# A pre-norm attention and mixture-of-experts layer: where GpSimd makes the router's constants, and three small moves

## The chip, the core and the metric

The kernel runs on one core of one Trainium2 chip. A core has five engines that run side by side, each through its own queue in order: TensorE (matmuls; PE in the profile, with its weight loads as PEld), VectorE (DVE), ScalarE (ACT), GpSimd (POOL) and SyncE (SP, which here only issues transfers). All data is float32; each matmul or transpose of the program shows as two instructions on TensorE. The metric is the device time of one execution in microseconds. Three executions of the kernel before took 1071.76, 1071.80 and 1072.09 us; the median is 1071.8.

## The reference

x has 4096 tokens of width 256. First an attention over normalized rows is added to x, then a mixture of experts over the normalized result:

```python
x = x + attn(layernorm(x), Qw, Kw, Vw)      # causal, one head of width 256
x = x + ffn(layernorm(x), W_in, b_in, W_gate, ...)

def attn(x, Qw, Kw, Vw):
    Q, K, V = x @ Qw, x @ Kw, x @ Vw
    scores = Q @ K.T / sqrt(256) + causal_mask
    return softmax(scores) @ V

def ffn(...):
    t = x @ W_in + b_in
    probs = softmax(t @ W_gate + b_gate)        # 8 experts
    topv, topi = top_k(probs, 2); topv /= topv.sum()
    mid = relu(t @ W1[e] + b1[e]); eout = mid @ W2[e] + b2[e]
    return (sum over the two experts of topv * eout) @ W_out + b_out
```

## The kernel before

The tokens are handled in 8 blocks of 512 (NB = 8), each of four tiles of 128 rows (TPB = 4); queries are handled in 16 groups of 256 (g from 0 to 15). The engines' order is chosen by a scheduler when the program is built, from what is ready by its own estimate. Two calls bind it: `tc.keep_in_program_order(ins)` puts an instruction behind the one that was traced before it on its engine, and `tc.issue_after(ins)` puts all that a block traces on the engine of `ins` behind `ins`. Neither is a wait for data.

**The start.** The transfers are issued by SyncE: the first block of x, W_in, W_gate, the rows of biases `brows` (b1 and b_in, 66 rows of 128), Vw, the other blocks of x, and small rows. Qw and Kw come by ScalarE's queue. TensorE first runs some matmuls of zeros (L115), then turns Qw and Kw (L494), which ScalarE copies to qwT and kwT (L495). `turn_weights` turns the biases (L191, pbias, copied to biasT) and W_in (L198, pwin, copied to winT). Then comes the first of two products pqk (L502), and between the two, as `turn_first`, W_in times W_gate (L229, pwg) and the turn of the first block's normalized rows (L306, pz), pinned in this order; then the second product, and `project(0)` (L522), which makes the first block's queries.

**Normalized rows.** VectorE takes statistics of a tile (L254, L255), GpSimd adds epsilon (L261) and raises to the power -1/2 (L262), and VectorE makes the rows z (L271), each a tensor_scalar of 128 x 256 with a mean and a factor per row. In the first block this is done in two pairs of tiles (`first_rows`), pinned; in the others in fours. The second block's statistics and factors (`stats0(1)`) are put behind the last copy of the first projection.

**GpSimd's constants.** Beside the identity and the mask, GpSimd makes what the router will need: a strictly triangular matrix `before` (a memset and an affine select), 24 small memsets (rank, first, number), `none`, two iotas and a memset (blocks, assign), and the tiles `empty` (128 x 256) and `zero` (128 x 256), from which SyncE fills the tables `slots` and the last part of `rows` in memory. The columns of ones of the eight value tiles v are made in `values` (L533), one memset each. Nothing binds the place of any of them on GpSimd.

**The attention.** For each group g, `scores(g)` makes the scores in chunks of 256 keys (L566, ps), with a running maximum on VectorE (top, L600 to L605). Its `finish` turns top (L612, pt), reduces it (L617, m), turns that to a row for all partitions (L622, pmax), subtracts (L626, L632) and takes exponents. `attend(g)` multiplies with v (L647, po), and its `between` runs parts of other work behind the matmuls of a chunk. The scores of group g + 1 are made ahead of attend(g). For g below CALM = 4 `finish` is called at once, free to be placed by the scheduler; from 4 on it stands in `between`, its first turn pinned.

**The end.** When the experts' parts are added up, `gather` turns each block's sums (L1215, pa) into two tiles of PSUM, ScalarE copies both (L1220, aT), and `leave` multiplies with W_out (L1229, pf).

Of the kernel before, what the change touches and what calls it, by code (L numbers as in the profile page):

```python
# [10 lines left out]
F32 = mybir.dt.float32  # L11
I32 = mybir.dt.int32
# [5 lines left out]
P = 128  # L18
# [19 lines left out]
def preln_attention_moe_kernel(  # L38
# [145 lines left out]
    biasT = const.tile([P, NBR], F32, tag="biasT", name="biasT")  # L184
    winT = []

    def turn_weights():

        ptb = ps_tr("pbias")
        tc.keep_in_program_order(  # L190
            nc.tensor.transpose(ptb[:, :NBR], brows, ident[:NBR, :NBR])  # L191
        )
        nc.scalar.copy(biasT, ptb[:, :NBR])
        winT.append(piece("winT", ND, D))
        pt = ps_o("pwin")
        for k in range(ND):
            for c in range(ND):
                done = nc.tensor.transpose(  # L198
                    pt[:, ts(k * ND + c, P)], win_sb[:, c, ts(k, P)], ident
                )  # L200
                tc.keep_in_program_order(done)
        nc.scalar.copy(winT[0].rearrange("p k d -> p (k d)"), pt)
# [46 lines left out]
    def freely(done):  # L249
        return done  # L250

    def ln_stats(k, t, keep=freely):
        st = stats.tile([P, 6], F32, tag="bn", name=f"bn{k}_{t}")
        keep(nc.vector.bn_stats(out=st, in_=xb[t // TPB][:, t % TPB, :]))  # L254
        keep(nc.vector.bn_aggr(out=lns[k][0][:, t, :], in_=st))  # L255

    def ln_rstd(k, b, tiles=TPB, keep=freely):

        s = ts(b, tiles)
        mv, rstd = lns[k]  # L260
        keep(nc.gpsimd.tensor_scalar_add(rstd[:, s, 0], mv[:, s, 1], EPS))  # L261
        keep(nc.gpsimd.tensor_tensor(rstd[:, s, 0], rstd[:, s, 0], half[:, s], ALU.pow))  # L262

    def ln_rows(k, b, fill=None):

# [21 lines left out]

    def first_rows():

        todo, keep = [], tc.keep_in_program_order  # L290
        z = ln_rows(0, 0, todo)
        for i in range(TPB // 2):
            for j in range(2):
                ln_stats(0, 2 * i + j, keep)
            ln_rstd(0, i, 2, keep)
        for do in todo:
            keep(do())
        return z
# [177 lines left out]
    def piece(name, *shape):  # L476

        return attn.tile([P, *shape], F32, tag="s", name=name, bufs=NS)
# [33 lines left out]
    def stats0(b):  # L512
        for t in range(b * TPB, (b + 1) * TPB):
            ln_stats(0, t)
        ln_rstd(0, b)

    def project(b):
        qT[b] = attn.tile([P, ND, TB], F32, tag="qT", name=f"qT{b}", bufs=2)
# [11 lines left out]
        return done  # L530

    def values(b):
        nc.gpsimd.memset(vb[b][:, :, D : D + 1], 1.0)  # L533
        for j in range(TPB):
            pv = ps_o(f"pv{b}_{j}")
            for c in range(ND):
                nc.tensor.matmul(
                    pv[:, :D],
                    lhsT=zT[b][:, j, c, :],
                    rhs=vw_sb[:, c, :],  # L540
                    start=(c == 0),
                    stop=(c == ND - 1),
                )
            nc.scalar.copy(vb[b][:, j, :D], pv[:, :D])
# [488 lines left out]
    z, gates = first_rows(), []  # L1033

    def turn_first():
        gates.append(prepare_gate())
        turn(0, 0, z, zT[0], True)

# [3 lines left out]
    with tc.issue_after(ready.ins):  # L1042
        nc.vector.tensor_copy(
            win_sb[:, :, D:], gates[0][:, : ND * NE].rearrange("p (c e) -> p c e", e=NE)
        )
        stats0(1)

    before = const.tile([P, P], F32, tag="before", name="before")
    make_upper_triangular(nc, before, 1.0, diag=False)

    rank = const.tile([P, TPB, NE], F32, tag="rank", name="rank")

    first = const.tile([P, TPB, NE], F32, tag="first", name="first")
    number = const.tile([P, NE], F32, tag="number", name="number")
    for e in range(NE):
        nc.gpsimd.memset(rank[:, :, e : e + 1], float(NE - e))
        nc.gpsimd.memset(first[:, :, e : e + 1], float(e * R))
        nc.gpsimd.memset(number[:, e : e + 1], float(e))
    none = const.tile([P, SU], I32, tag="none", name="none")
    nc.gpsimd.memset(none, NONE)  # L1060
    late_slot = const.tile([P, SU], I32, tag="late_slot", name="late_slot")
    blocks = const.tile([P, NFULL], F32, tag="blocks", name="blocks")
    nc.gpsimd.iota(
        blocks, [[1, NFULL]], base=0, channel_multiplier=0, allow_small_or_imprecise_dtypes=True
    )


    assign = const.tile([P, NT * TOPK + LINE], I32, tag="assign", name="assign")
    nc.gpsimd.memset(assign[:, NT * TOPK :], NONE)
    nc.gpsimd.iota(  # L1070
        assign[:, : NT * TOPK].rearrange("p (t k) -> p t k", k=TOPK),
        [[TOPK * P, NT], [1, TOPK]],
        base=0,
        channel_multiplier=TOPK,
    )
    empty = attn.tile([P, SB], I32, tag="s", name="empty", bufs=NS)
    nc.gpsimd.memset(empty, NONE)
    nc.sync.dma_start(
        out=slots.rearrange("(p n r) o -> p n (r o)", p=P, r=SB // LINE),
        in_=empty.unsqueeze(1).to_broadcast([P, NE * R // P * LINE // SB, SB]),  # L1080
    )
    zero = piece("zero", D)
    nc.gpsimd.memset(zero, 0.0)

    nc.sync.dma_start(
        out=rows[TOPK * (S - LATE * TB) :, :].rearrange("(t p) d -> p t d", p=P),
        in_=zero.unsqueeze(1).to_broadcast([P, TOPK * (LATE * TPB + 1), D]),
    )

    row, finish = scores(0)  # L1090
    finish()
# [4 lines left out]
    for g in range(NT // KU):  # L1096
        b, q = divmod(g, QPB)

        between = {}
        nxt = None  # L1100
        if g + 1 < NT // KU:

            nxt, finish = scores(g + 1, fill)
            if g < CALM:
                finish()
            else:
                between[min(g - 2, 4)] = [partial(finish, True)]
        fill = []
        if q == 0 and b == NB - 1:

            assert not puts
            early = seen
            tables["a"] = plan("a", early, NFULL, SB, 0)
            for n in range(AHEAD + 1):
                got[n] = fetch_rows(work[n])
        if q == 0 and b > 0:

            def send(behind=False, b=b):
                nonlocal lg
                lg = enter(b - 1, z1T, attn, behind)  # L1120

            if b - 1 >= EASY[1]:
                between[5] = [partial(send, True)]
        if q == 0 and b == NB - 1:

            def fetch_first():
                for n in range(AHEAD):
                    got[n] += fetch_weights(work[n])

            def find():  # L1130
                nonlocal seen
                seen = route(b - 1, lg, seen, attn, True)
                while puts:
                    puts.pop(0)()

            between[6], between[11] = [fetch_first], [find]
            weighed = AHEAD
        elif g == 0:
            turn(0, 1, ahead, zT[1])
        late = q == 1 and 0 < b <= EASY[1]  # L1140
        if late:
            send()
        attend(g, row, between)
        row = nxt
        if q == 0 and b + 1 < NB:
            project(b + 1)
            values(b + 1)
        if late or q == 0 and EASY[1] < b < NB - 1:
            seen = route(b - 1, lg, seen, attn)
        if q == 0 and b + 2 < NB:  # L1150
            stats0(b + 2)
            todo = []
            todo += turn_todo(zT[b + 2], ln_rows(0, b + 2, todo))
            if b + 2 >= EASY[0]:
                fill += todo
            else:
                for do in todo:
                    do()
        if q == QPB - 1:
            ln_rstd(1, b)  # L1160
            z1T = attn.tile([P, TPB, ND, P], F32, tag="z1T", name=f"z1T{b}", bufs=1)
            todo = []
            rows1 = ln_rows(1, b, todo)
            if b < NB - 1:
                todo += turn_todo(z1T, rows1)
            if EASY[1] <= b < NB - 1:
                fill += todo
            else:
                for do in todo:
                    do()  # L1170
# [36 lines left out]
    def gather(b):  # L1207

        pts = [ps_tr(f"pa{b}_{c}") for c in range(ND)]
        if b > 0:  # L1210
            add_up(b)
        for i in range(2):
            for j in range(HT):
                for c in range(ND):
                    nc.tensor.transpose(  # L1215
                        pts[c][:, ts(i * HT + j, P)], accs[b, i][:, j, ts(c, P)], ident
                    )
        aT = [piece(f"aT{b}_{c}", TB) for c in range(ND)]
        for c in range(ND):
            nc.scalar.copy(aT[c], pts[c])  # L1220
        return aT

    def leave(b, aT):
# [127 lines left out]
```

## Time and profile before

| what | us |
|---|---|
| median of three executions | 1071.8 |
| the profiled execution | 1071.8 |
| its span, first to last instruction | 1070.0 |
| TensorE busy | 1062.0 (99%) |
| VectorE busy | 675.2 (63%) |
| ScalarE busy | 332.4 (31%) |
| GpSimd busy | 237.8 (22%) |

The profile is that of one execution. A busy time is the union of an engine's instructions; those of TensorE overlap, and their ends are modelled, so that what TensorE loses is better read from the starts of its instructions. A timeline line gives the start and the duration in us, the engine, the line of the code, the operation, what it writes and reads, the shapes and how many instructions were merged into the line; in brackets stands the idle time of the engine ahead of it and what ended it. Small differences of time in this text are taken from the starts of single instructions in the same trace.

### The profile page before, as it was taken

Reading aid. Unit: us, or ns where it says so; the run is one execution under the profiler, and the core shown is the slowest. Engines: PE = TensorE matmul, PEld = TensorE weight load, DVE = VectorE, ACT = ScalarE, POOL = GpSimd, SP = SyncE. Lnnn points to the kernel's source line nnn. Section 1 sums busy time; section 2 is a strip of 40 time slices with the busy share of each in tenths; the row PEclk is TensorE's granted clock in tenths of the full one; section 3 lists DMA queues with packets and bytes.
Section 4 is the critical chain, followed back from the end, with each engine's and each line's share of the span. In section 5 each row is a group of like instructions: output and inputs, shape, how many; then the busy total and the mean of one; then the engine's idle time right before and its main releaser. Section 6 shows DMA issues by size and latency. Waiting matters only on the chain. (4 is left out here: it accounts for less than half of the span.)

```text
span 1070.0 us, 15840 instructions
## 1 busy us (share of the span) xinstructions
PE 1062.0 (99%) x4973; PEld 882.8 (83%) x4973; DVE 675.2 (63%) x2158; ACT 332.4 (31%) x734; POOL 237.8 (22%) x289
## 2 busy tenths in 40 slices
PE   9999999999999999999999999999999999999998
PEld 6788888888888888888888887777878787777887
DVE  5877667564655546254665634858588786767636
ACT  2232233322432323242402221232323332323254
POOL 2102123202201110200223323232322322313110
PEclk9999999999999999999999999999999999999999
DMA  9431212121021011001655339887889796969285
GB/s 313 104 59 37 61 21 51 19 54 23 7 48 22 8 21 39 3 2 20 203 170 182 120 107 319 260 290 266 280 270 313 259 330 219 330 217 331 72 296 191
DMA packets 177994, 158.80 MB, mean 148 GB/s; under 512 B 82157, under 2 KB 157874, under 8 KB 177908
## 3 DMA queue, kind: packets, MB, share of 16 engines
q1 hardware_dynamic: 168980, 139.67, 41.8%
q0 software_dynamic: 8384, 17.58, 5.1%
q8 instruction: 40, 0.66, 0.2%
q10 hardware_dynamic: 544, 0.52, 0.1%
q14 instruction: 46, 0.38, 0.1%
HBM read 124.79 MB, written 26.38 MB: 141 GB/s over the span
## 5 line engine op out<-in xcount | busy, mean ns | idle before, releaser
L647 PE MATMUL po<-v,s 128*128 128x257 f32 x1056 | 237.9, 380 | 0.0
L566 PE MATMUL ps<-qT,zT 128*128 128x256 f32 x1088 | 233.3, 374 | 0.0
L566 PEld LDWEIGHTS ps<-qT,zT 128*128 128x128 f32 x1088 | 203.1, 190 | 28.0 <-issue 1.0
L647 PEld LDWEIGHTS po<-v,s 128*128 128x128 f32 x1056 | 197.2, 190 | 26.7
L575 ACT COPY s<-ps 128x512 f32<-128x512 f32 x120 | 70.2, 585 | 171.9 <-PE ps L566 129.1
L1004 PE MATMUL pe_a<-w_a,mid_a 128*128 128x256 f32 x544 | 121.6, 380 | 0.0
L935 PE MATMUL pm_a<-hT_a,w_a 128*128 128x256 f32 x544 | 120.0, 379 | 0.0
L1004 PEld LDWEIGHTS pe_a<-w_a,mid_a 128*128 128x128 f32 x544 | 102.6, 190 | 19.0 <-issue 5.6
L944 ACT ACTIVATE mid_a<-pm_a,c_a 128x256 f32<-128x256 f32 x136 | 63.8, 472 | 166.6 <-PE pm_a L935 125.7
L935 PEld LDWEIGHTS pm_a<-hT_a,w_a 128*128 128x128 f32 x544 | 103.4, 190 | 14.1
L581 DVE TENSOR_TENSOR mx<-ps,mx 128x512 f32<-128x512 f32 x91 | 62.9, 692 | 81.9 <-ACT s L575 75.4
L629 ACT ACTIVATE s<-s 128x512 f32<-128x512 f32 x120 | 72.3, 630 | 100.2 <-DVE s L626 100.2
L392 POOL DMA_INDIRECT slots<-assign,ati x64 | 63.5, 992 | 132.7 <-DVE ati L391 118.5
L915 DVE STREAM_TRANSPOSE hT_a<-h_a 32x128 f32<-32x128 f32 x272 | 82.2, 302 | 5.5 <-issue 1.7
L626 DVE TENSOR_TENSOR s<-s,pmax 128x512 f32<-128x512 f32 x120 | 73.1, 681 | 7.3 <-PE pmax L622 7.3
L1014 POOL DMA_INDIRECT parts<-y_a,slot_a x34 | 34.2, 1005 | 155.8 <-DVE y_a L1012 126.3
L907 DVE STREAM_TRANSPOSE mid_c<-raw_c 32x256 f32<-32x256 f32 x128 | 55.8, 436 | 1.9
L1004 PE MATMUL pe_b<-w_b,mid_b 128*128 128x256 f32 x256 | 56.8, 380 | 0.0
L935 PE MATMUL pm_b<-hT_b,w_b 128*128 128x256 f32 x256 | 56.6, 379 | 0.0
L1004 PEld LDWEIGHTS pe_b<-w_b,mid_b 128*128 128x128 f32 x256 | 48.5, 190 | 9.4 <-issue 3.1
L935 PEld LDWEIGHTS pm_b<-hT_b,w_b 128*128 128x128 f32 x256 | 48.6, 190 | 6.6
L944 ACT ACTIVATE mid_b<-pm_b,c_b 128x256 f32<-128x256 f32 x64 | 30.1, 471 | 63.0 <-PE pm_b L935 62.1
(281 smaller groups left out, 1169.3 us busy)
## 6 DMA issues: line engine op xcount, KB each, us to landing
w_a<-in_L_ffn_W_dram SPq DMA_DIRECT2D x68, 512.0 KB
w_d<-in_L_ffn_W_dram SPq DMA_DIRECT2D x48, 512.0 KB
w_c<-in_L_ffn_W_dram SPq DMA_DIRECT2D x32, 512.0 KB
w_b<-in_L_ffn_W_dram SPq DMA_DIRECT2D x32, 512.0 KB
rows<-hr SPq DMA_DIRECT2D x16, 512.0 KB
yp<-parts SPq DMA_DIRECT2D x14, 512.0 KB
x<-in_L_attn_x_dram SPq DMA_DIRECT2D x7, 512.0 KB
z1T<-z SPq DMA_DIRECT2D x112, 32.0 KB
```

The source lines that it names most:

```text
L392: put = nc.gpsimd.indirect_dma_start(out=slots, out_offset=bass.IndirectOffsetOnAxis(ap=ati, axis=0), in_=assign[:, TOPK * (b * TPB + j) + ...
L566: nc.tensor.matmul(ps[:, u * QB + lo : (u + 1) * QB], lhsT=zT[kt // TPB][:, kt % TPB, d, :], rhs=qT[b][:, d, q * QB + lo : (q + 1) * QB], ...
L575: nc.scalar.copy(flat, ps)
L581: done = nc.vector.tensor_tensor(mx, ps, old, ALU.max)
L626: nc.vector.tensor_tensor(s, s, pm[:, :QB].unsqueeze(1).to_broadcast([P, KU, QB]), ALU.subtract)
L629: nc.scalar.activation(s, s, AF.Exp)
L647: nc.tensor.matmul(po[u][:, : D + 1], lhsT=ss[c][:, k, ts(u, P)], rhs=vb[kt // TPB][:, kt % TPB, :], start=(kt == 0), stop=(kt == g * KU + u),
L907: pin(do())
L915: pin(do())
L935: nc.tensor.matmul(pm[:, :SB], lhsT=w1[c][:, ts(f, P)], rhs=hT[:, c, :], start=(c == 0), stop=(c == ND - 1),)
L944: nc.scalar.activation(mid[f // 2][:, f % 2, :], pm[:, :SB], AF.Relu, bias=c1[:, f : f + 1])
L1004: nc.tensor.matmul(pe[ts(j, rest), :D], lhsT=mid[f][:, ts(u, P)][:, ts(j, rest)], rhs=w2[f // (NF // 2)][:, f % (NF // 2), :], start=(f == 0),
```

## The change

- `turn_weights` is split. The biases' turn, now `turn_biases`, is called at the head of `turn_first`: behind the first product pqk and ahead of W_in times W_gate.
- `stats0` and `ln_rstd` return their last instruction, the power on GpSimd. All the router's constants, the fills of slots and rows, and the memsets of v's ones (now eight in one place, taken out of `values`) are traced under `issue_after` of the second block's power. The fills are SyncE's and so aren't bound by it, but they read what GpSimd makes there.
- For g = 2, `finish` of the fourth group (g + 1 = 3) isn't called at once but in `between[2]`: behind the last matmuls of attend(2), with its first turn pinned.
- In `gather`, for the first block alone, the second of the two copies is VectorE's.

```diff
-    def turn_weights():
-
+    def turn_biases():
         ptb = ps_tr("pbias")
         tc.keep_in_program_order(
             nc.tensor.transpose(ptb[:, :NBR], brows, ident[:NBR, :NBR])
         )
         nc.scalar.copy(biasT, ptb[:, :NBR])
+
+    def turn_weights():
+
         winT.append(piece("winT", ND, D))
...
+    def in_order(done):
+        tc.keep_in_program_order(done)
+        return done
+
...
-        keep(nc.gpsimd.tensor_tensor(rstd[:, s, 0], rstd[:, s, 0], half[:, s], ALU.pow))
+        return keep(
+            nc.gpsimd.tensor_tensor(rstd[:, s, 0], rstd[:, s, 0], half[:, s], ALU.pow)
+        )
...
-        todo, keep = [], tc.keep_in_program_order
+        todo, keep = [], in_order
...
-        ln_rstd(0, b)
+        return ln_rstd(0, b)
...
     def values(b):
-        nc.gpsimd.memset(vb[b][:, :, D : D + 1], 1.0)
...
     def turn_first():
+        turn_biases()
         gates.append(prepare_gate())
         turn(0, 0, z, zT[0], True)
...
-        stats0(1)
-
-    before = const.tile([P, P], F32, tag="before", name="before")
-    make_upper_triangular(nc, before, 1.0, diag=False)
...
+        second = stats0(1)
+
+    with tc.issue_after(second.ins):
+        for v in vb:
+            nc.gpsimd.memset(v[:, :, D : D + 1], 1.0)
+        before = const.tile([P, P], F32, tag="before", name="before")
+        make_upper_triangular(nc, before, 1.0, diag=False)
...
-            if g < CALM:
+            if g < CALM and g != 2:
                 finish()
             else:
-                between[min(g - 2, 4)] = [partial(finish, True)]
+                between[2 if g == 2 else min(g - 2, 4)] = [partial(finish, True)]
...
         for c in range(ND):
-            nc.scalar.copy(aT[c], pts[c])
+            if b == 0 and c:
+                nc.vector.tensor_copy(aT[c], pts[c])
+            else:
+                nc.scalar.copy(aT[c], pts[c])
         return aT
```

The lines between `before` and the fill of `rows` are the same on both sides, indented.

## The prediction

> **What bounds the kernel.** First the page: TensorE is busy 1062.0 us of a span of 1070.0 us and its clock is never reduced, so the end moves only by what TensorE waits for. (The profiled execution took 1071.8 us, which is also the median: 1.8 us lie outside the span, and a change of the span is a change of the time.) So next the list of TensorE's waits; its columns are the total, the number and the longest, in us.
>
> ```profile
> PE pbias L191 <- DMA brows<-in_L_ffn_b_dram: 1.1, 1, 1.1
> ...
> PE pt L612 <- DVE top L603: 1.0, 1, 1.0
> PE pf L1229 <- ACT aT L1220: 0.6, 1, 0.6
> ```
>
> These three waits are at 6.6, 51.3 and 1032.2 us, and each is touched by one part of the change. The fourth part, GpSimd's constants, is seen in the timeline of the start (start, duration, engine, line, out<-in):
>
> ```profile
> 6.89 1.48 DVE L271 TENSOR_SCALAR z<-x,ln0mv,ln0rstd 128x256 f32<-128x256 f32 x2
> 7.01 0.36 POOL L261 TENSOR_SCALAR ln0rstd<-ln0mv 128x2 f32<-128x2 f32 x1 [0.56 <-DVE past L441]
> 7.31 0.10 POOL L1056 MEMSET rank<- 128x4 f32 x1
> ...
> 8.12 0.09 POOL L1060 MEMSET none<- 128x2 int32 x1
> 8.18 0.24 POOL L1063 IOTA blocks<- 128x17 f32 x1
> ...
> 8.60 0.71 POOL L262 TENSOR_TENSOR ln0rstd<-ln0rstd,half 128x2 f32<-128x2 f32 x1
> ...
> 9.35 1.45 DVE L271 TENSOR_SCALAR z<-x,ln0mv,ln0rstd 128x256 f32<-128x256 f32 x2 [0.98 <-POOL ln0rstd L262]
> ```
>
> The second pair of factors has its addition at 7.01 but its power only at 8.60: 28 constants stand between. And VectorE's two rows take 1.48 and 1.45 us a pair, where three take 1.05 us later on. The query of that line says the same (minimum/median/maximum, ns):
>
> ```profile
> L271 DVE TENSOR_SCALAR z<-x,ln0mv,ln0rstd x32: 396/405/1153, 6.9 to 336.9; 128x256 f32<-128x256 f32 x32
> ```
>
> Exactly two of the rows are long (1153 and 1129 ns), the two that overlap runs of GpSimd constants. The first ends at 8.36, just after the run of memsets passes over into the iota (8.18); the second begins at 9.35 and ends at 10.48, 0.15 us after the last memset.
>
> **Part 1, biases' turn behind the first product; part 2, constants out of the first block.** Before, TensorE ends the turn of Kw near 6.6, waits for brows to 7.71, spends 0.09 us on it, and has W_in's turn at 7.80, the first product pqk at 8.24, pwg at 9.10 and the turn of z at 9.99. After, W_in's turn comes first; the DMA records signal the last part of win at 6.81, so it runs 6.85 to 7.29 (four turns of 0.109). The product needs kwT, whose copy ends at 7.28, so it starts at 7.33 instead of 8.24. Four matmuls of 0.215 and the biases' turn (brows is there since 7.7) put pwg at 7.33 + 0.86 + 0.09 = 8.28, 0.82 earlier. The turn of z is at 8.28 + 0.89 = 9.17. It took 1.13 us because the last rows came late; eight turns of 0.109 are 0.87. Are the rows there? Without the constants the power runs 7.45 to 8.17, and rows three and four end near 8.95: yes. So the second product starts at 10.04 where it stood at 11.12: **1.08 us gained**, carried on by the projection, since zT's copies follow the turn as before. Bounds: 0.8 (if rows are late by another reason) to 1.1.
>
> **Part 2, the other end: where the constants go.** They now follow the second block's power on GpSimd. Before:
>
> ```profile
> 18.67 1.04 POOL L262 TENSOR_TENSOR ln0rstd<-ln0rstd,half 128x4 f32<-128x4 f32 x1
> ...
> 19.75 0.41 DVE L271 TENSOR_SCALAR z<-x,ln0mv,ln0rstd 128x256 f32<-128x256 f32 x1 [0.62 <-POOL ln0rstd L262]
> ...
> 20.08 0.28 DVE L605 TENSOR_TENSOR top<-top,s 128x128 f32<-128x128 f32 x1
> 20.28 1.05 DVE L271 TENSOR_SCALAR z<-x,ln0mv,ln0rstd 128x256 f32<-128x256 f32 x3
> 20.41 0.14 PEld L612 LDWEIGHTS pt<-ident,top 128*128 128x128 f32 x1 [0.52 <-DVE top L605]
> ```
>
> The four rows wait for the same power. GpSimd's next instruction starts with no gap (9.29 after a power that ended at 9.31), VectorE's first row 0.04 us later. So 2.5 us of constants (7.31 to 8.61, 9.29 to 10.33, and 0.19 for the memset at 5.55) start just ahead of the rows. Behind the first row on VectorE stands L605, for which TensorE's second pt waits with no margin; behind the other rows stands the reduction m (L617, 21.25), for which pmax waits (21.90, margin 0.2).
>
> How long is a row held? The Trainium skill, page "SBUF — State Buffer", section "Who interferes with whom", says that a VectorE tensor_scalar in a two-port mode and a GpSimd instruction exclude each other, the first to issue keeping the port for its whole instruction; it also says that an operation with two inputs in SBUF, as L605 is, isn't held by a mere write. It speaks against this change. Held for one memset (0.1 us), four rows would lose at most some 0.4 us. The rows say more: a row waited for the whole run, 28 constants or 0.9 us, and lost 0.73 us; small memsets follow each other every 0.033 us and leave no opening. I take the row. In program order the run up to the first iota is v's 0.3, the mask's 0.45, then 0.85: the first row of block 1 ends some 1.7 us after the power instead of 0.45, L605 and the second pt are late by 1.25, and m, behind rows that meet empty and zero (0.55 more), by some 1.3 to 1.5. **1.3 us lost**; by one memset a row it would be 0.1 to 0.4. Ends: 0 (the order puts L605 ahead of the rows; then even the 0.28 us that TensorE loses there now would go) and 2.3 (all constants pass ahead of the first row).
>
> The constants' users are later: v's ones are read at 25.59, rank and the others by routes after 60 us. On SyncE the two fills (0.65 and 4.41 us of issue) wait for empty and zero until about 21; the biases' store (7.15 us) may pass in front. Even all three from 21 are through by 33.5, and the next user of that queue, the sixteen zT moves, starts at 37.57. The fills' 4.5 MB at the 370 GB/s of the start need 12 us, to about 35. Nothing is charged; without these 4 us of cover, there are 5 more before the projection at 55.44 reads zT.
>
> **Part 3, the fourth queries' maxima.** The timeline of TensorE there:
>
> ```profile
> 48.99 2.33 PE L647 MATMUL po<-v,s 128*128 128x257 f32 x10
> ...
> 52.31 0.29 DVE L605 TENSOR_TENSOR top<-top,s 128x128 f32<-128x128 f32 x1
> ...
> 52.34 0.33 PE L612 MATMUL pt<-ident,top 128*128 128x128 f32 x1 [1.01 <-DVE top L603]
> ```
>
> Ten of the 22 po matmuls run, then TensorE waits; by starts it stands 1.17 us. After, pt is behind all 22: they end at 48.99 + 22 x 0.217 = 53.77, and top is done at 52.61, 1.16 us of margin. Next late are m (0.43) and pmax: TensorE has eight pq matmuls of 0.43 to put in between. **1.15 us gained.** Ends: 1.2, and -0.7, by the third rival.
>
> **Part 4, one copy of the first sums on VectorE.** The last stage:
>
> ```profile
> 1032.17 1.07 ACT L1220 COPY aT<-pa 128x512 f32<-128x512 f32 x2 [5.61 <-PE pa L1215]
> ...
> 1032.80 1.59 PEld L1229 LDWEIGHTS pf<-wout,aT 128*128 128x128 f32 x8 [0.80 <-ACT aT L1220]
> ```
>
> The wait is for the first of the two copies, which ends at 1032.75; pf starts at 1032.80. That one stays on ScalarE. The second ends at 1033.24 and is wanted at 1033.34, so it wasn't waited for; on VectorE, idle there, a copy of such a tile takes 0.69 us and ends near 1033.03. **Nothing gained**, 0.1 either way.
>
> **Sum.** +1.08 - 1.3 + 1.15 + 0 = 0.9 us off the span: 1069.1, time **1070.9 us**. TensorE has no slack elsewhere, so what is gained reaches the end. A change under 0.2% (2.1 us) is what a measurement of this kernel can't tell from none.
>
> **Rivals.** *All stalls go*: the rows slip between the constants, or L605 stands ahead of them. 1.08 + 1.15 + 0.0 to 0.28 = 2.2 to 2.5 us: 1069.4. For it: VectorE has some room (idle 0.6 us before 19.75); against it: both overlapping rows of the trace were held. *The order isn't what the text says*: the scheduler leaves a part where it was, part 3 say: 0.9 - 1.15 = -0.2, 1072.0. Against it: an edge on the engine's own order binds the scheduler. *Slower*: pt now comes at the end of attend, when po is complete too, so VectorE may take the residual update first: two reciprocals, two updates, two statistics with their aggregates, 2.4 us by the rows at 56.66 to 59.1. If pmax stands after two pq (0.86) on TensorE, it waits 2.4 + 0.4 - 0.9 = 1.9 us; with part 3's 1.15 that is -0.7, and with the head's -0.2, 0.9 us slower: 1072.7. It decides from where VectorE's queue ahead of m is longer than the pq ahead of pmax. For it: nothing pins either. Against it: at 41.2 m stood ahead of the same reciprocals.
>
> **Chances.** Forecast 0.52 (its own range 1070.2 to 1071.5), all stalls gone 0.27, order unchanged 0.08, slower 0.13. The range 1069.2 to 1072.4 takes in the first rival and part of the last. Faster by over 2.1 us needs nearly all of the first rival: 0.24. Slower by over 2.1 us needs twice the third rival's price, or what I don't see: 0.07. Within: 0.69.
>
> **What would show it.** Right: the first pqk near 7.35, rows one to four of block 0 all near 0.41 us; in the first rows of block 1 one or more over 1 us, and the second pt waiting over a microsecond for L605; no wait of pt near 52; pf still waiting 0.56 for aT. Wrong: rows of block 1 at 0.41 (first rival), or pmax waiting for m near 54 (third).

## The result, and the profile after

| | before | after |
|---|---|---|
| median of 17 executions each, us | 1071.88 | 1074.06 |
| lowest to highest, us | 1071.67 to 1073.83 | 1071.82 to 1076.41 |
| ratio, 95% interval | | 1.0019 [1.0012, 1.0026] |
| the profiled execution, us | 1071.8 | 1071.82 |
| its span, us | 1070.0 | 1070.0 |

The changed kernel is 2.2 us slower in the median, where the forecast was 0.9 us faster. Yet its profiled execution takes as long as that of before, to a few hundredths. So there are two questions: why the span isn't shorter, and why most executions are longer than the profiled one.

**The first question** is answered in the profile. TensorE's waits (total, number, longest, in us):

```profile
PE pt L619 <- DVE top L607: 2.2, 1, 2.2
...
PE pf L1243 <- ACT aT L1234: 0.6, 1, 0.6
...
PE pwin L200 <- DMA win<-in_L_ffn_W_in_dram: 0.3, 1, 0.3
```

The wait for the biases and the wait near 51 us are gone. A wait of 0.3 us for W_in and one of 2.2 us for the first group's maxima have come. The timeline of the start, after:

```profile
6.86 0.66 PE L200 MATMUL pwin<-ident,win 128*128 128x128 f32 x4 [0.30 <-DMA win<-in_L_ffn_W_in_dram]
7.36 1.06 PE L510 MATMUL pqk<-kwT,qwT 128*128 128x256 f32 x4
...
8.26 0.73 DVE L279 TENSOR_SCALAR z<-x,ln0mv,ln0rstd 128x256 f32<-128x256 f32 x2 [0.61 <-POOL ln0rstd L269]
8.32 1.01 PE L231 MATMUL pwg<-wgate,winT 128*128 128x8 f32 x8
...
9.18 1.07 PE L314 MATMUL pz<-ident,z 128*128 128x128 f32 x8
10.09 1.03 PE L510 MATMUL pqk<-kwT,qwT 128*128 128x256 f32 x4
```

The head is as forecast: the second product starts at 10.09 instead of 11.12, and two rows of z take 0.73 us together where they took 1.45 to 1.48. Then the second block's factors, with the constants behind them:

```profile
17.50 1.03 POOL L269 TENSOR_TENSOR ln0rstd<-ln0rstd,half 128x4 f32<-128x4 f32 x1
18.50 0.32 POOL L1058 MEMSET v<- 128x4 f32 x8
18.57 1.77 DVE L279 TENSOR_SCALAR z<-x,ln0mv,ln0rstd 128x256 f32<-128x256 f32 x2 [1.48 <-POOL ln0rstd L269]
...
18.89 0.10 POOL L1067 MEMSET rank<- 128x4 f32 x1
...
19.75 0.24 POOL L1074 IOTA blocks<- 128x17 f32 x1
...
20.26 0.27 DVE L601 TENSOR_TENSOR s<-ps,mask 128x128 f32<-128x128 f32 x1
...
20.82 0.47 DVE L279 TENSOR_SCALAR z<-x,ln0mv,ln0rstd 128x256 f32<-128x256 f32 x1
21.21 0.27 DVE L601 TENSOR_TENSOR s<-ps,mask 128x128 f32<-128x128 f32 x1
21.41 0.28 DVE L607 COPY top<-s 128x256 f32<-128x256 f32 x1
21.61 0.40 DVE L279 TENSOR_SCALAR z<-x,ln0mv,ln0rstd 128x256 f32<-128x256 f32 x1
21.74 0.33 PE L619 MATMUL pt<-ident,top 128*128 128x128 f32 x1 [2.16 <-DVE top L607]
```

Two things are to be seen. The first of the two rows takes 1.37 us by its own record: it ends at 19.94, when the memsets have passed over into the iota (19.75). And **VectorE's order is another one**. Before, mask, mask and top stood ahead of every row of the second block, the first of which started at 19.75:

```profile
17.92 0.26 DVE L594 TENSOR_TENSOR s<-ps,mask 128x128 f32<-128x128 f32 x1
...
18.63 0.29 DVE L594 TENSOR_TENSOR s<-ps,mask 128x128 f32<-128x128 f32 x1 [0.20 <-ACT s L598]
...
18.84 0.28 DVE L600 COPY top<-s 128x256 f32<-128x256 f32 x1
```

Now two rows stand ahead of the first mask and a third ahead of the second. VectorE is idle from 17.10 to 18.57, because the row at its head waits for the power; the first mask doesn't need it (with the constants elsewhere, in an experiment below, it runs at 16.95). In the fourth group's place the wait has gone:

```profile
49.99 4.94 PE L654 MATMUL po<-v,s 128*128 128x257 f32 x22
...
53.31 0.29 DVE L612 TENSOR_TENSOR top<-top,s 128x128 f32<-128x128 f32 x1
...
54.77 0.38 PE L619 MATMUL pt<-ident,top 128*128 128x128 f32 x2
```

By the starts of the same TensorE instructions in the two traces, the balance of this execution is: 1.03 us gained in the head and 1.23 near 51 us (1.17 of it the wait that is gone); 2.04 lost at the first group's two turns pt, and 0.24 lost between 650 and 661 us in the experts' part. At these turns TensorE now stands for 2.32 us, all at the first, where it stood for 0.28, all at the second. (Such a wait "by starts" is the distance between the starts of two instructions, less what it is when nothing stalls.) The sum is 0, as the two spans say.

**The second question** is answered by the granted clock of all executions. TensorE's mean clock is 1.0 in only 3 of the 17; in the others it is 0.997 or 0.998. A mean of 0.998 over 1072 us is some 3.4 us at half the clock. The profiled execution is one of the three.

### The profile page after: what moved, and what is told of

It is laid out like the page before. It is cut to its first block, busy times and chain, and to the rows that moved or that the text cites. A ratio compares the mean times of both kernels' runs of the same rounds, so it can differ in the third digit from the quotient of the medians.

```text
span 1070.0 us, 15838 instructions
## 1 busy us (share of the span) xinstructions
PE 1061.4 (99%) x4973; PEld 882.6 (82%) x4973; DVE 676.1 (63%) x2159; ACT 332.1 (31%) x733; POOL 238.6 (22%) x289
```

## The experiments

Each is a change of the changed kernel unless it says otherwise. The times of the kernel before that stand beside it were taken together with it, on the same chip. A ratio is to that kernel, with its 95% interval in brackets.

### The clock

**The changed kernel again**, to catch an execution with the lower clock in a profile.

> The changed kernel again, for a trace of one of its usual executions. Clock theory: its times lie between 1071.8 and 1076.4 us as before; where the time is over 1073 the granted TensorE clock is at half for some 3.4 to 7 us, and the lost time is about the time at half clock that falls on matmuls (2 to 4.5 us); the half clock begins within a few us of the long wait for top near 21 us. Rival, transfers: the lost time is spread over the mixture of experts as waits for weights or rows, and the clock is the same in slow and quick executions.

Measured: 1074.35 us (20 executions), before 1072.01 (58), ratio 1.0017 [1.0010, 1.0024]. This profile shows the lower clock. The table of stretches, one line for each kernel (stretch, its length, then busy time and number of instructions of each engine, clock, DMA share and GB/s); first the execution with clock 1.0:

```profile
21.93:28.75 6.82, 6.82 (x41) 5.78 (x41) 4.59 (x16) 1.37 (x4) 0.00 (x0) 1.00 0.99 331
```

and that of this run:

```profile
21.93:28.75 6.82, 6.82 (x20) 5.55 (x21) 2.06 (x7) 1.10 (x3) 0.00 (x0) 0.50 1.00 333
```

Behind the wait of pt, which ends at 21.89, TensorE runs at half speed from 21.93 for 6.83 us: 20 instructions where there were 41, a score matmul every 0.427 us instead of 0.216. The busy time is the same in both lines; only the number of instructions and the clock tell them apart. Half a clock for 6.83 us costs 3.4 us. By their mean clock of 0.998, most other executions have 3.41 us of it, which cost 1.7. All 37 executions of the changed kernel, sorted by clock:

| mean clock | executions | median, us |
|---|---|---|
| 1.0 | 4 | 1072.34 |
| 0.998 | 27 | 1074.13 |
| 0.997 | 6 | 1075.93 |

Of the 58 executions of the kernel before, one is below 1.0 (0.998, 1075.99 us). At clock 1.0 the changed kernel is near the kernel before (1072.0 at clock 1.0 here); the steps of 1.8 and 3.6 us fit the two lengths of the stretch. The rest of this profiled execution's 4.5 us over the first one is 1.05 us of a wait of pm_a for mid_a at 656 us, and a first wait that is 0.2 us longer. The clock's row on the profile's page (PEclk, in slices of 27 us) shows none of this: it reads 9 in every slice here too.

**The wait filled.** The block's value products are traced first, and five matmuls of zeros stand where TensorE waits; everything else stays, the constants and VectorE's late maxima too.

```diff
     row, finish = scores(0)
-    finish()
     values(0)
+    fill = ps_tr("fill")
+    for _ in range(5):
+        done = nc.tensor.matmul(fill[:, :QB], lhsT=zeros, rhs=..., start=True, stop=True)
+        tc.keep_in_program_order(done)
+    finish(True)
```

> The changed kernel with five matmuls of zeros (2.2 us) put between the values of block 0 and the first turn of the maxima, so that TensorE works while it would wait for top; their result is used by nothing. The wait itself isn't shortened. Clock theory: the clock stays at 1.0 in all executions, the times lie close together at 1071.8 to 1072.3 us, about 2 us under the changed kernel's median. Rival, the long wait alone or the transfers cost the time: median stays near 1074 with a spread of several us.

Measured: 1072.61 us (13), ratio 1.0008 [1.0000, 1.0017], clock 1.0 in all 13. The first pt still starts late:

```profile
19.50 2.32 PE L1105 MATMUL fill<-zeros 128*128 128x256 f32 x10
22.00 0.33 PE L619 MATMUL pt<-ident,top 128*128 128x128 f32 x1 [0.18 <-DVE top L607]
```

Work that computes nothing makes the kernel 1.7 us faster than it was without it (1074.35). What it takes away is TensorE's idle time, so the drop follows from that idle time and not from lateness. The times didn't lie as close together as expected: they reach from 1072.12 to 1075.03 us, all at clock 1.0, so there is a loss in some executions that isn't the clock's.

**Idle time without constants beside it.** It could still be that the GpSimd constants are needed for the drop. So the constants go to the start, as in "Constants at the very start" below, and VectorE's order is held as in the changed kernel. A row of the second block is then written again ahead of the masks (the same values): once for the first kernel, three times for the second. With a row that the scheduler adds, 4 and 7 rows stand ahead of the first mask, where the order alone has 2. The value products are traced ahead of pt, and the biases' preparation (what the expectation calls the fill of the slots) and the second group's scores are held behind it, so that nothing steps into the gap.

```diff
...
+    held = [do() for do in todo[:2]]
+    for _ in range(1):          # 3 in the second kernel
+        held.append(todo[1]())
+        tc.keep_in_program_order(held[-1])
+    with tc.issue_after(held[-1].ins):
+        row, finish = scores(0)
     values(0)
+    finish(True)
...
```

> e5_order with two z rows of block 1 written twice more (the same values) ahead of the masks and the fill of the slots moved behind the first pt, so that TensorE waits longer for block 1's scores while GpSimd makes nothing beside them. Both theories: wait of the first pt by starts about 1.7 us (1.06 in e5 and some 0.65 more), so 1070.5 + 0.7 = 1071.2 us. Theory (the idle time itself lowers the granted clock, from a little under the 2.3 us of the changed kernel): clock 1.0 in most executions, 0.998 in few or none. Rival (the drop needs GpSimd's memsets beside VectorE, not the idle time): clock 1.0 in all.

> As e9, with two more repeats: wait of the first pt by starts about 2.4 us, as long as in the changed kernel (2.3 to 2.5), with no constants of GpSimd beside it. Theory (the idle time itself lowers the clock): the clock shows 0.998 in most executions, a half-clock stretch of 3.41 us begins behind the wait, and the median is 1070.5 + 1.3 + 1.8 = 1073.6 us, within 0.6. Rival (the drop needs GpSimd's memsets): clock 1.0 in all and 1071.8 us.

Measured, the shorter: pt waits 1.71 us by starts; 1073.24 us (11), before 1071.99 (24), ratio 1.0008 [0.9999, 1.0018]. Four executions at clock 1.0 have a median of 1071.26, as summed; six at 0.998 have 1073.41, one at 0.997 has 1076.61. The longer: pt waits 2.71 us, 0.3 more than meant; 1074.87 us (8), ratio 1.0021 [1.0010, 1.0031]; two at 1.0 (1072.97), five at 0.998 (1074.91), one at 0.997. So its time lies above the range expected. Its profile has the half clock, with no GpSimd instruction from 19.2 to 35 us:

```profile
20.20:22.77 2.57, 0.03 (x1) 0.00 (x0) 2.37 (x10) 0.64 (x2) 0.00 (x0) 1.00 1.09 387
24.06:27.47 3.41, 3.41 (x11) 2.65 (x10) 0.62 (x2) 0.63 (x3) 0.00 (x0) 0.50 1.09 386
27.50:31.00 3.50, 3.50 (x24) 3.18 (x24) 2.43 (x6) 0.80 (x2) 0.00 (x0) 1.00 1.08 381
```

The rival falls. The theory's direction holds and its threshold is lower than I had put it: 1.7 us already lowered the clock in 7 of 11 executions where few or none were expected.

**The same at another place.** The constants at the start, and ScalarE copies the first tile of sums of the last stage (L1234) four times instead of once, so that pf and what follows wait at 1030 us.

```diff
+            for _ in range(3 if b == 0 and c == 0 else 0):
+                nc.scalar.copy(aT[c], pts[c])
```

> e3 with ScalarE making the first copy of the first block's sums four times instead of once, the same values each time: TensorE is idle for 0.73 + 3 x 0.585 = 2.5 us near 1030 us, far from the start, from GpSimd and from the rows. Clock theory: the idle time costs 1.75 us, and in most executions a half clock of 3.4 or 6.8 us follows it, another 1.7 or 3.4 us: median 1070.3 + 1.75 + 1.7 = 1073.7 us, clock 0.998 in most. Rival (the half clock belongs to the start, where the clock has only just come up): clock 1.0, 1072.0 us.

Measured: 1074.18 us (11), before 1071.82 (33), ratio 1.0019 [1.0010, 1.0028]. Nine of 11 are below clock 1.0; the two at 1.0 took 1072.4. The profile has three gaps on TensorE (1.75, 0.68 and 0.73 us by starts, all between 1030.4 and 1034.0, two of them because the extra copies also delay the sums behind them), then 3.41 us of half clock:

```profile
1034.42:1037.83 3.41, 3.41 (x12) 2.66 (x11) 0.79 (x2) 2.13 (x5) 0.00 (x0) 0.50 1.00 338
```

So it isn't a property of the start, and an idle time in pieces will do.

### What makes the first pt wait

**Constants at the very start.** All that part 2 moves is traced ahead of the first block's rows instead, so that GpSimd makes it before there are factors to make; the fill of slots is pinned.

```diff
+    for v in vb:
+        nc.gpsimd.memset(v[:, :, D : D + 1], 1.0)
+    before = const.tile([P, P], F32, tag="before", name="before")
...
     z, gates = first_rows(), []
...
-    with tc.issue_after(second.ins):
-        for v in vb:
...
```

> The changed kernel with GpSimd's constants traced ahead of the first block's factors, in its idle time from 1.9 to 5.4 us; nothing else differs. Port and order theory: all rows of blocks 0 and 1 take 0.41 us, the first pt no longer waits, the head keeps its 1.0 us and the fourth maxima their 1.15 us: 1069.6 us (1069.3 to 1069.9), clock 1.0, spread under 0.5. Rival, the gain of the parts was an illusion of one trace: 1071 to 1072 us.

Measured: 1070.28 us (14), before 1072.01, ratio 0.9982 [0.9974, 0.9990], clock 1.0 in all; span 1067.8. VectorE's order is that of the kernel before, the first pt doesn't wait and the second stands 0.27 us, and the head and part 3 keep their gain. The span is 2.2 us under that of before: 0.97 in the head and 1.23 near 51 us.

The profiled execution is the fastest of the 14; the median is 0.7 us above the 1069.6 expected, and the times reach to 1073.03 where a spread under 0.5 was expected. The other profiles show a likely reason. TensorE starts at half speed, a zeros matmul every 0.43 us, and comes up to full speed at 3.90 to 7.18 us, differently in each profile. Where it comes up by 5.26 us, in seven profiles with the changed head and the constants out of it, the second product starts at 10.05 to 10.17. Where it comes up at 6.77 to 7.18, in four others, the product starts at 10.69 to 10.89, because the turn of Kw is still slow. Here is that turn in the changed kernel, and in an experiment below (without part 3):

```profile
5.96 0.60 PE L502 MATMUL pkwT<-ident,kw 128*128 128x128 f32 x4
```

```profile
6.46 0.96 PE L502 MATMUL pkwT<-ident,kw 128*128 128x128 f32 x4
```

So in executions of the second kind the head gains only 0.2 to 0.4 us over the 11.12 of before. That the kernel before loses little there is an estimate: in those four profiles the copy of Kw ends by 7.8 to 8.05, and the product of before starts at 8.24. No run tried this apart.

**Without part 2.** The constants are free again, as before; parts 1, 3 and 4 stay.

```diff
-    with tc.issue_after(second.ins):
-        for v in vb:
-            nc.gpsimd.memset(v[:, :, D : D + 1], 1.0)
+    before = const.tile([P, P], F32, tag="before", name="before")
...
     def values(b):
+        nc.gpsimd.memset(vb[b][:, :, D : D + 1], 1.0)
```

> The changed kernel without its second part: the constants free to stand anywhere, as before the change. Theory: the constants stand between the first block's factors again, two rows take over 1.1 us, so that the head gains 0.1 to 0.8 us instead of 1.0; no long wait at pt; the fourth maxima keep 1.15 us: 1070.1 us (1069.8 to 1070.7), clock 1.0. Rival (part 1 alone makes the long wait): 1072 to 1074 us.

Measured: 1070.81 us (21), ratio 0.9989 [0.9983, 0.9996], clock 1.0 in 20 (0.999 in the other). VectorE's order is as before; the turn of z waits 0.60 us for its last rows, so a part of the head's gain is missing. Part 2 is what made the change slower: without it the same kernel is 3.5 us faster (1074.35 against 1070.81).

**The order without the constants beside it.** Constants at the start, but VectorE held to the changed kernel's order: two rows, mask, row, mask, top.

```diff
-    row, finish = scores(0)
...
+    ahead = ln_rows(0, 1, todo)
+    held = [do() for do in todo[:2]]
+    with tc.issue_after(held[1].ins):
+        row, finish = scores(0)
...
```

> The constants in GpSimd's early idle time, as in e3, but VectorE's order at block 1's rows forced to that of the changed kernel: two rows ahead of the first mask, a third ahead of the second. It has the changed kernel's order without its contention. If the order alone made the long wait: pt waits 2.3 us, rows take 0.41. If order and port share it: the rows take 0.41 us each, pt waits 1.2 us (1.0 to 1.4), some 1.2 us over e3, and, as the idle time stays under that of the kernel before at 51 us, the clock stays at 1.0: 1070.9 to 1071.6 us. If the port alone: no wait at pt, as e3, 1070.3.

Measured: 1070.54 us (11), before 1071.82 (33), ratio 0.9989 [0.9980, 0.9998], clock 1.0 in all. The rows are at their own speed:

```profile
18.52 0.73 DVE L279 TENSOR_SCALAR z<-x,ln0mv,ln0rstd 128x256 f32<-128x256 f32 x2 [1.47 <-POOL ln0rstd L269]
19.17 0.28 DVE L601 TENSOR_TENSOR s<-ps,mask 128x128 f32<-128x128 f32 x1
...
20.10 0.28 DVE L607 COPY top<-s 128x256 f32<-128x256 f32 x1
```

pt stands 1.06 us by starts. Of the changed kernel's 2.32 us, 0.27 is lost at these turns with the old order too, 0.79 is the order, and the other 1.26 is what VectorE loses beside the constants: 1.04 of it in the two rows ahead of the mask (1.77 against 0.73), 0.16 in the copy of binc (0.44 against 0.28). The time is a little under the range expected; the two spans, 1068.5 and 1067.8, differ by 0.7, as the order's share says. 1.06 us of waiting leaves the clock alone.

**The constants there without the order.** The constants stay where the change puts them; the second block's rows are held behind the first reduction, so that they meet no constant and stand ahead of no mask.

```diff
...
-    ahead = ln_rows(0, 1)
+    with tc.issue_after(reduced[0].ins):
+        ahead = ln_rows(0, 1)
```

> The changed kernel with block 1's rows put behind the reduction m of the first maxima on VectorE; the constants stay behind block 1's power. Theory: constants and rows may still meet, but nothing that TensorE wants soon stands behind the rows; pt waits under 0.4 us, the clock stays at 1.0, as e3: 1070.3 us (1069.6 to 1070.8). Rival (constants there are harmful in themselves, by the transfers that they free or by masks and tops held too): 1072 or more.

Measured: 1070.38 us (11), ratio 0.9987 [0.9978, 0.9996], clock 1.0 in 10 of 11. The wait of pt is 0.72 us by starts, and 0.22 more at the second; more than I had expected, because now another instruction stands where the rows stood:

```profile
19.25 0.32 POOL L1060 MEMSET v<- 128x4 f32 x8
19.28 1.42 DVE L609 COPY top<-s 128x256 f32<-128x256 f32 x1
...
20.73 0.29 DVE L614 TENSOR_TENSOR top<-top,s 128x128 f32<-128x128 f32 x1
```

The copy of top takes 0.28 us elsewhere. It begins just behind the first of the memsets and ends at 20.70, 0.20 us after the first iota starts (20.50). So this copy is held as the rows were.

### Part 3, and a better version

**Without part 3**, constants at the start: the fourth group's finish is called at once again.

```diff
-            if g < CALM and g != 2:
+            if g < CALM:
                 finish()
             else:
-                between[2 if g == 2 else min(g - 2, 4)] = [partial(finish, True)]
+                between[min(g - 2, 4)] = [partial(finish, True)]
```

> e3 without the third part: the fourth queries' maxima free to be placed, as before the change. Theory: pt waits about 1.0 us near 51 us again, 1.15 us by starts, and all of it reaches the end: 1070.3 + 1.15 = 1071.4 us, clock 1.0. Rival (the wait only moves to the next stage): as e3, 1070.3.

Measured: 1071.06 us (11), before 1071.82, ratio 0.9993 [0.9984, 1.0002]; the wait of pt near 51 us is back with 1.15 us by starts. The kernel with part 3 ran on another chip; by the two ratios to the kernel before (0.9982 and 0.9993) part 3 is worth 0.11%, 1.2 us, as its wait says. The two intervals overlap, so it is the wait in the trace that shows this, and the time only agrees.

**Both copies cut.** Constants at the start, and the copies of the first sums (part 4) are each cut at column 128, so that pf can start on the first piece.

```diff
+            by = nc.vector.tensor_copy if b == 0 and c else nc.scalar.copy
+            for cut in (slice(0, P), slice(P, TB)) if b == 0 else (slice(0, TB),):
+                by(aT[c][:, cut], pts[c][:, cut])
```

> e3_first with the copies of aT of block 0 cut at column 128, half on ScalarE and half on VectorE for each. Theory: pf's wait for aT falls from 0.56 us to about 0.25, all else as in e3, so 1070.0 us (0.3 under e3's 1070.3), clock 1.0. Rival (the wait ends with the other of the two copies, or VectorE takes its half late): the wait stays at 0.5 or more, and the time at 1070.3.

Measured: 1070.30 us (11), before 1071.99, ratio 0.9982 [0.9973, 0.9991]. The step is there:

```profile
1031.48 1.35 PE L1242 MATMUL pf<-wout,aT 128*128 128x256 f32 x5 [0.25 <-ACT aT L1233]
```

From the first pa to the last the profile counts 29.94 us where the uncut kernel has 30.21. The time doesn't show it: this execution loses 1.2 us to waits of pm_a near 650 us, as the second profile of the changed kernel loses 1.05 there; the uncut kernel's profile and that of before don't have them. 0.3 us of gain is below what these medians can tell, so the cut version and the uncut one stand level, both faster than both kernels of the case.

## Why the prediction was wrong, step by step

- **Head, "1.08 us gained": right in this profile.** 1.03 measured. The first product was put at 7.33, pwg at 8.28, the turn of z at 9.17, the second product at 10.04; they stand at 7.36, 8.32, 9.18 and 10.09. What the sum doesn't have is that the clock comes up at another time in each profile: where it comes up late, only 0.2 to 0.4 is left.
- **Part 3, "1.15 us gained": right.** The wait of 1.17 is gone, and TensorE is 1.23 earlier. The third rival's fear was half true: VectorE did take one update of the residual ahead of m, but the two pq matmuls covered it.
- **Part 4, "nothing gained": right.** pf waits 0.57 us for the same copy.
- **Part 2, "1.3 us lost": the first step that failed.** It was worked out as "L605 and the second pt are late by 1.25", with masks and top ahead of the rows as they stood in the trace of before. That order was free, and building the changed program gave another. So the first pt was late, not only the second, and by more than the step's price: 2.04 us over before. The constants' share alone, 1.26 us in the difference of two kernels, is near the number, so the hold of the rows was rightly foreseen and the order was not. The upper end of the step's range, 2.3, was given with another mechanism. With this the sum is 1.03 + 1.23 - 2.04 = 0.2 us, which the experts' part took back.
- **"Its clock is never reduced, so the end moves only by what TensorE waits for": the second, and the one that made the kernel slower.** That was read from a kernel whose longest wait behind the first 8 us is 1.2 us, and carried over to one with a longer wait. The prediction had no term for the clock. A wait of 2.3 us doesn't cost 2.3 us: in 33 of 37 executions it brought 3.41 or 6.83 us of half clock with it, 1.7 or 3.4 us more. The Trainium skill, page "TensorE: Matmul & The Clock Gate", section "Part 1: The HAM clock gate", says that TensorE falls to half rate after an idle window of about 3.4 us; by that figure too the wait of 2.3 us would have been safe. Here the measurement decides: waits of 1.7 to 2.7 us were enough, in most executions.
- **The first rival, "all stalls go", 1069.4:** it was this change's best case, and what the constants at the start came to in the profile: a span 2.2 us down, as its sum said. By the ratio, 0.9982, it is 1.9 us in the median.
- **"A change under 0.2% (2.1 us) is what a measurement of this kernel can't tell from none": too wide.** The 17 executions of each kernel tell 0.19% from none, with an interval of 0.07% to either side.

What stays open: where exactly the boundary of the idle time lies (1.06 us: none of 11; 1.7: 7 of 11; 2.3 to 2.5: 33 of 37; 2.7: 6 of 8), why the scheduler turned VectorE's order round in the changed kernel, why one execution of the kernel before has the lower clock, and what decides whether the waits near 650 us appear in an execution.

## What to carry to other kernels

A stall of TensorE has two prices: its length, and the half clock that may follow it. Here waits of 1.06 us did no harm and waits of 1.7 us did; short waits close together add up. Where a long one can't be avoided, matmuls that compute nothing were cheaper than waiting. The clock's row on the profile's page is too coarse to show such a stretch; the mean clock of each execution shows it. Work that is "off the path" on GpSimd belongs where VectorE has no copy or tensor_scalar to issue, which in this kernel is at the start, and not behind the instruction that VectorE also waits for. And an order that nobody pinned is not carried over from the trace of before: a step that is costed by it should name the edge that holds it, or price the other order too.

## What the hardware showed that I had not expected

- The clock moves on a grid. In the three profiles with a drop, the time from one change of the clock to the next, counted from its first rise, is a whole number of 3.413 us: 17.067 (5), 6.827 (2), 3.413 (1) and 1044.478 (306), for example. That agrees with the window of 3413 ns, running free of the program, that the Trainium skill gives on the page "TensorE: Matmul & The Clock Gate", section "Part 1: The HAM clock gate". But the window ahead of the drop need not be idle throughout. By starts it holds 2.50 us of idle time in the second profile of the changed kernel (18.52 to 21.93), 2.67 in the longer of the idle kernels (20.65 to 24.06) and 2.75 in the kernel that waits at 1030 us. In the nine profiles without a drop that record the clock, no window on the grid holds more than 1.92 (the first profile of the changed kernel; 1.59 in the shorter idle kernel). So where the grid falls would decide whether the same wait lowers the clock in one execution and not in the next. With the grid placed worst, a window of the shorter idle kernel would hold 2.25 us, its short waits included, and one of the kernel with the order alone 1.39. A bound of some 2 us in a window would fit these; that is an estimate from the profiles and wasn't tried apart.
- Beside a run of back-to-back memsets VectorE's copy or tensor_scalar ended only with the run, not after one memset. A row took 1.15 us before and 1.37 after instead of 0.41, a copy 1.42 instead of 0.28, and all three end 0.18 to 0.20 us after the first iota starts. A tensor_tensor beside the affine select took its usual 0.27. The Trainium skill's page "SBUF — State Buffer", section "Who interferes with whom", which the prediction set against the row, has the pair blocked for a whole instruction; here VectorE was held for a whole run of instructions. The runs show the hold, and that it goes when the constants go elsewhere; that the shared port is its cause is what the page says.
